# Layer 0's rows of sequences 3 to 7 turned by 32x32 blocks on VectorE and an exchange through memory

## The chip, the cores and the metric

The kernel runs on one core of a Trainium2 chip. The time is the device time of one execution in microseconds (us); of several runs the median is given. A trace of one profiled execution stands beside it: every instruction of the five engines (TensorE or PE, VectorE or DVE, ScalarE or ACT, GpSimd or POOL, SyncE or SP) with its start, its length and what it waited for. DMAs are issued from the queues of SyncE, ScalarE and GpSimd ("SPq", "ACTq", "POOLq" in the trace). All data are 32-bit floats.

## What is computed

Eight sequences (B = 8) of 128 positions with 512 features go through two layers. Layer 0 multiplies each sequence by an adapter matrix that its id picks, and adds a feed-forward step with two of eight low-rank experts. Layer 1 is attention over a paged cache of 512 keys plus the 128 new ones (32 query heads, 8 key heads, with normalised and rotated queries and keys), followed by a gated low-rank feed-forward step with 16 of 64 experts.

```python
x = x + _L0_ffn_ref(_L0_cond_ref(x, L0_cond_weight, itok_B_3_7), ...)
x = x + _L1_ffn_ref(_L1_cond_ref(x, L1_cond_Wq, L1_cond_Wk, L1_cond_Wv, L1_cond_Wo, ...), ...)

# in _L1_cond_ref
q = jnp.einsum('bsd,ed->bse', x, Wq).reshape(bsz, seqlen, HQ, D)
k = jnp.einsum('bsd,ed->bse', x, Wk).reshape(bsz, seqlen, HK, D)
v = jnp.einsum('bsd,ed->bse', x, Wv).reshape(bsz, seqlen, HK, D)
```

The change concerns what lies between the two layers: the projections of layer 1 (these three products) need x with the features on the partitions, and layer 0 leaves it with the positions on the partitions. So each sequence's 128x512 result has to be turned (transposed) once.

## The kernel before

**The order of the work is written by hand.** On each engine, and in each DMA queue, instructions run in the order in which the source issues them. An instruction that waits holds up all behind it in the same queue. Semaphores between queues are set by the framework from the reads and writes of tiles; a tile that takes a buffer of a pool waits until the last reader of the tile before it in that buffer is through.

**Layer 0** is the loop `for t in range(B)` from line 585. Iteration t computes the adapter product of sequence t (`l0_adapter`, lines 486 to 504, into PSUM and by `cT` on ScalarE back to SBUF), finishes the experts of sequence t-1 (`l0_turn_low` and `l0_experts`, lines 549 to 571, where L558 on TensorE needs `lowT`, which ScalarE copies from PSUM) and starts the base product of sequence t (`l0_base`, L512 and L517, which need `cT`). `l0_experts` leaves two things: the rows `x1` go to memory (L561, read again at the end of the kernel), and the rows scaled by a power of two go into the tile `xb` (L568 on ScalarE). `l0_turn` (lines 573 to 579), called two iterations later for t from 2 to 7 and twice after the loop, turns `xb` with four transposes on TensorE (L577) into a PSUM bank (`bank("q")`, for the last two sequences one of `banks`) and copies it on ScalarE into the operand tile `xo` (L579). The pool of `xb` has three buffers, so `l0_load_x(t + 2)` (L392, from the queue of SyncE) takes the buffer of sequence t-1.

From iteration 4 on, products of layer 1 (`project_whole`, L292) stand between those of layer 0 wherever their operands are there: for sequences 0 and 1 in the loop, for sequence 2 after it and in iteration 0 of layer 1, for sequence 3 from iteration 1. Sequences 4 to 7 enter through `sums_x` (GpSimd, iterations 2 and 5). `project_whole` puts its result into bank "q" or "kv", and ScalarE copies it out (L299). `norms` (ScalarE, with two steps on GpSimd), `rotate` (VectorE, lines 317 to 350) and `transpose_qk` (TensorE, L358) make queries and keys of the first units; `sums_q` (VectorE, L163) combines weights. SyncE's queue carries the loads of x, of weights and of key pages (`gather`, L194), and the writes of `x1`.

**Layer 1** is `for u in range(NU + 3)` with 64 units (a sequence and a key head each). Iteration u computes scores of unit u (L798, L801), a masked minimum and exponent (L811 on VectorE, L822 on ScalarE), a normalisation (L828 on GpSimd) and a turn of the probabilities by 32x32 blocks on VectorE (L833). `exchange_out` writes the blocks to memory from the queues of SyncE and ScalarE, `exchange_in` in the next iteration reads them back, so that blocks from different partitions change places; `values` (L880) uses them in iteration u+2, `evict_o` (L891) and `output` (L902) follow in iteration u+3. Queries and keys of unit 3 and later go the same way (L784, `px<-xo` and `qkb<-px`).

The pool `yp` (tag "ya", three buffers) holds `bias`, `ang` and `kk` in layer 0 and output rows in layer 1.

Of the kernel before, what the change touches and what calls it, by code (L numbers as in the profile page):

```python
# [9 lines left out]
F32 = mybir.dt.float32  # L10
# [6 lines left out]
P = 128  # L17
B = 8
S = 128
DM = 512  # L20
NC = DM // P
# [12 lines left out]
QD = P // 32  # L34
# [23 lines left out]
def adaln_ffn_kernel(  # L58
# [25 lines left out]
    nc = tc.nc  # L84
# [262 lines left out]
    def rotate(u):  # L347
        rotate_q(u)
        rotate_k(u)
# [14 lines left out]
        qkT_t[u] = home.rearrange("p (h s) -> p h s", h=NH)  # L364


    with ExitStack() as l0:
        w0p = l0.enter_context(tc.tile_pool(name="w0p", bufs=1))
        p2 = l0.enter_context(tc.tile_pool(name="l0_2", bufs=2))
# [25 lines left out]
        glw = w0p.tile([P, NC, E0 + E0 * R0], F32, name="glw")  # L395
        bww = w0p.tile([P, NC, DM], F32, name="bww")
        lb = w0p.tile([P, DM], F32, name="lb")
        bias = yp.tile([P, DM], F32, tag="ya", name="bias")

        wt_home = {}  # L400
        pairs = [wp.tile([P, 7, 2 * HW], F32, tag="wqkv", name=f"wqkv_{i}", bufs=GH) for i in (0, 1)]
# [171 lines left out]
        def l0_turn(b):  # L573
            x1 = state.pop(b)
            tp = banks(f"x1tp_{b}") if b >= B - 2 else bank("q", f"x1tp_{b}")
            for c in range(NC):
                nc.tensor.transpose(tp[:, c * S : (c + 1) * S], x1[:, c * P : (c + 1) * P], ident)  # L577
            half = xo[:, b // 2, b % 2 * 2 : b % 2 * 2 + 2]
            nc.scalar.copy(half.rearrange("p x c s -> p (x c s)"), tp[:, :DM])  # L579


        idle = bank("q", "idle")
# [2 lines left out]
        for t in range(B):  # L585
            l0_adapter(t, True)
            if t >= 1:
                l0_turn_low(t - 1)
            l0_adapter(t, False)
            if t + 3 < B:  # L590
                l0_load(t + 3)
            if t + 2 < B:
                l0_load_x(t + 2)
            if t in (3, 4):
                load_q(t - 3)
            if 2 <= t <= 5:
                gather(0, (t - 2) * 4, (t - 1) * 4)
            elif t > 5:
                gather(1, (t - 6) * 4, (t - 5) * 4)
            if t >= 2:  # L600
                l0_turn(t - 2)

            if t == 5:
                project_whole(0, 0, 0, 1)
                norms(0)
            if t == 6:
                project_whole(0, 0, 1, 0)
            if t == 7:
                project_whole(0, 1, 1, 1)
                transpose_qk(0)  # L610
            if t >= 1:
                l0_experts(t - 1)
            l0_base(t)
            if t == 0:
                l0_rows()
            if 1 <= t <= 4:
                l0_angles(t - 1)
            if t in (3, 6):
                gather_v(t // 3 - 1, 0, LC)
            if t in (5, 6):  # L620
                make_tables(t - 5)
            if t == 4:
                project_whole(0, 0, 0, 0)
            if t == 5:
                project_whole(0, 0, 1, 1)
                sums_q(0, 3, 2)
            if t == 6:
                project_whole(0, 1, 0, 1)
                rotate(0)
                norms(2)  # L630
                sums_q(0, 4)
            if t == 7:
                project_whole(0, 1, 0, 0)
                norms(1)
        for g in range(GH):
            load_o(g)
        l0_turn_low(B - 1)
        project_whole(0, 1, 1, 0)
        l0_turn(B - 2)
        rotate(1)  # L640
        l0_experts(B - 1)
        project_whole(1, 0, 0, 0)
        transpose_qk(1)
        norms(3)
        rotate(2)
        l0_turn(B - 1)
        project_whole(1, 0, 0, 1)
        transpose_qk(2, wt_7.rearrange("p c n -> p (c n)")[:, : NH * S])
        rotate(3)


    fw_t, zg_t = {}, {}
# [99 lines left out]
    with ExitStack() as l1:  # L752
# [223 lines left out]
        def iteration(u):  # L976

            on = lambda v: 0 <= v < NU
            fb = LAST.get(u)
            r, group = u % 16, (u // 16 + 1) * GH  # L980
            f = room(fb) if fb is not None else None

            if u % 4 == 3:
                k, j, four = (u + 5) // 4, 0, True
            elif u % 4 == 0:
                k, j, four = (u + 4) // 4, 0, False
            elif u % 4 == 1:
                k, j, four = (u + 3) // 4, 1, True
            else:
                k, j, four = (u + 2) // 4, 1, False  # L990
            slots = ()
            if 2 < u and k < NU // 4:
                slots = (1, 2, 6) if four else (4, 5, 3)
            st = u // GH
            pages = on(u) and 1 < st + 1 < NQ * B
            first, end = ((0, 10), (10, NPP))[u % GH]
            if pages:
                gather(st + 1, first, first + 3)
            if on(u - 1):
                exchange_in(u - 1)  # L1000
            if pages:
                gather(st + 1, first + 3, end)
            if pages:
                gather_v(st + 1, u % GH * LC // GH, (u % GH + 1) * LC // GH)
            if on(u + 3) and u % GH == 1:
                make_tables(units[u + 3][0])
            if u % GH == 0 and B <= st - 1 < NQ * B:
                load_y(st - 1)
            if on(u - 3):
                evict_o(u - 3)  # L1010
            if u >= NU and fb is not None:
                yT_t[fb] = f_turn(fb, *f)
            if u > NU:
                z = u - NU - 1
                z_turn(z, bank("q" if z else "kv", f"ztp_{z}"), lambda n, shape: y_home[
                    z
                ].rearrange("p (c s) -> p c s", c=NC))
            for h in range(REP):
                if on(u):
                    scores(u, h)  # L1020
                    mask_exp(u, h)
                    if h > 0:
                        normalize(u, h - 1)

                    if h == 1:
                        if u == 2:
                            rotate(4)
                        elif u == 3:
                            sums_q(1, 3, 2)
                        elif u == 4:  # L1030
                            sums_q(1, 4, 1)
                        elif r in (10, 11, 12, 13) and u < NU - 8:
                            sums_q(group + r // 12, *((3, 2), (4, 1))[r % 2])
                    if h == 2:
                        new_pb(u)
                        if u + 2 in range(3, NU):
                            blocks_qk(u + 2, u)
                    if h > 1:
                        blocks(u, h - 2)
                    if h == 1 and u == NU - 5:  # L1040
                        f_fold(f[1])
                    if h == 2 and fb is not None:
                        yT_t[fb] = f_turn(fb, *f)
                if on(u - 3):
                    output(u - 3, h)
                if h > 0 and slots:
                    project(k, j, slots[h - 1 : h])

                if (u, h) in WHOLE:
                    project_whole(1, *WHOLE[u, h])  # L1050
            if on(u - 3):
                add_output(u - 3)
            if on(u + 1) and (u + 1) % GH == 0:
                make_mask(units[u + 1][0])
            if u + 1 in range(3, NU):
                heads_qk(u + 1)

            if u < NU - 8:
                if r in (8, 9, 10, 11):
                    load_q(group + r // 10, r % 2, r % 2 + 2)  # L1060
                if r in (12, 13):
                    load_o(group, r % 2 * 2, r % 2 * 2 + 2)
            if 16 < u < NU and r in (1, 2):
                load_o(group - 1, r * 2 - 2, r * 2)
            if NU - 8 < u < NU - 2:
                f_weights(u - NU + 7)
            if u == 2:
                sums_q(0, 1)
            if on(u):
                normalize(u, REP - 1)  # L1070
            if u == 0:
                norms(4)
            elif 4 < u + 3 < NU:
                norms(u + 3)
            if on(u):
                blocks(u, REP - 2)
                blocks(u, REP - 1)
                exchange_out(u)
            if 4 < u + 3 < NU:
                rotate(u + 3)  # L1080
                if four and slots:
                    project(k, j, (7,))

            if u in (2, 5, 7, 9):
                sums_x({2: 2, 5: 3, 7: 0, 9: 1}[u])
            if u == NU - 14:
                t = wp.tile([P, 4 * DM], F32, tag="wo", name="y_home", bufs=GH + 1)
                y_home.update({b: t[:, b * DM : (b + 1) * DM] for b in range(4)})
            if u == NU - 6:
                rooms()  # L1090
            if fb is not None:
                f_gate(fb, *f_project(fb, yT_t.pop(fb), *f), *f)
            if on(u - 2):
                values(u - 2)
# [160 lines left out]
```

## Time and profile before

| what | value |
|---|---|
| median of three runs | 1243.18 us (1242.82 to 1249.42) |
| the profiled execution's own time | 1245.7 us |
| its span, first to last instruction | 1243.9 us |
| mean granted TensorE clock | 0.998 |
| moved by DMA | 298.99 MB, mean 240 GB/s |
| four transposes of one sequence (L577), each | 273 ns median |
| ScalarE's copy of one turned sequence (L579) | 592 ns median |
| layer 0's loop and tail | from the start to about 114 us |

"Busy" is the time in which an engine works on an instruction. TensorE's instructions are pipelined: a transpose is listed with 273 ns, though in a row of four the next one starts well before that. So the cost of a row of matmuls is read from its start to the start of what follows. The granted clock is the share of TensorE's full speed.

### The profile page before, as it was taken

Reading aid. Unit: us, or ns where it says so; the run is one execution under the profiler, and the core shown is the slowest. Engines: PE = TensorE matmul, PEld = TensorE weight load, DVE = VectorE, ACT = ScalarE, POOL = GpSimd, SP = SyncE. Lnnn points to the kernel's source line nnn. Section 1 sums busy time; section 2 is a strip of 40 time slices with the busy share of each in tenths; the row PEclk is TensorE's granted clock in tenths of the full one; section 3 lists DMA queues with packets and bytes.
Section 4 is the critical chain, followed back from the end, with each engine's and each line's share of the span. In section 5 each row is a group of like instructions: output and inputs, shape, how many; then the busy total and the mean of one; then the engine's idle time right before and its main releaser. Section 6 shows DMA issues by size and latency. Waiting matters only on the chain.

```text
span 1243.9 us, 15998 instructions
## 1 busy us (share of the span) xinstructions
PE 1225.7 (99%) x3847; PEld 651.1 (52%) x3847; DVE 901.9 (73%) x2045; ACT 506.5 (41%) x1457; POOL 590.9 (48%) x687
## 2 busy tenths in 40 slices
PE   8999899999999999999999999999999999999998
PEld 7765455554555555545555545554555555555444
DVE  3546788888877777788877777788777777777522
ACT  1334444444444444444444444444444444443211
POOL 2443565576544444565545545555555444543100
PEclk9999999999999999999999999999999999999999
DMA  8822777788877887788878878888888877787512
GB/s 302 304 78 94 229 234 245 245 274 281 269 243 245 272 258 239 259 295 278 269 248 267 264 221 258 294 272 267 257 268 262 255 243 233 246 261 269 179 51 85
DMA packets 205505, 298.99 MB, mean 240 GB/s; under 512 B 84643, under 2 KB 117156, under 8 KB 204516
## 3 DMA queue, kind: packets, MB, share of 16 engines
q1 hardware_dynamic: 173812, 205.58, 52.6%
q10 hardware_dynamic: 18720, 52.32, 12.0%
q0 software_dynamic: 12880, 40.08, 9.7%
q8 instruction: 31, 0.51, 0.2%
q14 instruction: 62, 0.51, 0.1%
HBM read 183.54 MB, written 114.36 MB: 239 GB/s over the span
## 4 chain that ended last, share of the span: by engine, by line
PE 89%; DMA 4%; DVE 2%; ACT 1%; issue 1%; POOL 1%; SPq 1%; ACTq 0%; DVEq 0%; POOLq 0%
PE o L880 19%; PE p L259 19%; PE y L902 17%; PE s L798 16%; PE s L801 4%; PE bp L517 2%; PE op L1147 2%; PE p L292 2%; PE cp L495 2%; PE fz L701 2%; DMA kt<-in_kc 1%; DMA bww<-in_base_w 1%; DMA px<-pb 1%; PE cp L512 1%; DMA pT<-px 1%
## 5 line engine op out<-in xcount | busy, mean ns | idle before, releaser
L828 POOL TENSOR_SCALAR p<-p,den 128x640 f32<-128x640 f32 x256 | 211.8, 827 | 424.4 <-DVE den L827 423.8
L822 ACT ACTIVATE p<-p,low 128x640 f32<-128x640 f32 x256 | 211.9, 828 | 436.3 <-DVE den L827 295.6
L811 DVE CUSTOM_DVE_ANT_0 p<-s,mask,rs 128x640 f32<-128x640 f32 x256 | 223.5, 879 | 108.8 <-PE s L801 106.1
L259 PE MATMUL p<-wqkv,xo 128*128 128x384 f32 x784 | 280.5, 487 | 0.0
L902 PE MATMUL y<-wo,oT 128*128 128x512 f32 x512 | 262.8, 598 | 7.6 <-ACT oT L891 7.4
L798 PE MATMUL s<-kt,qkT 128*128 128x512 f32 x504 | 258.9, 595 | 1.5 <-DVE low L811 0.8
L880 PE MATMUL o<-pT,vt 128*128 128x512 f32 x512 | 230.2, 593 | 0.0
L833 DVE STREAM_TRANSPOSE pb<-p 128x640 f32<-128x640 f32 x256 | 211.0, 824 | 16.9 <-POOL p L828 16.9
L259 PEld LDWEIGHTS p<-wqkv,xo 128*128 128x128 f32 x784 | 149.1, 190 | 139.8 <-issue 72.3
L801 PEld LDWEIGHTS s<-qkT 128*128 128x128 f32 x504 | 96.2, 191 | 121.0 <-issue 121.0
L880 PEld LDWEIGHTS o<-pT,vt 128*128 128x128 f32 x512 | 97.5, 190 | 110.1 <-issue 95.0
L204 POOL DMA_INDIRECT vt<-in_vc,vrow x128 | 136.3, 1065 | 37.4 <-issue 28.2
L798 PEld LDWEIGHTS s<-kt,qkT 128*128 128x128 f32 x504 | 95.4, 191 | 96.7 <-issue 54.0
L308 ACT ACTIVATE sq<-c 128x128 f32<-128x128 f32 x320 | 98.8, 309 | 8.1
L314 POOL TENSOR_TENSOR rs<-ss,mhalf 128x5 f32<-128x5 f32 x64 | 99.5, 1554 | 5.3
L801 PE MATMUL s<-qkT 128*128 128x128 f32 x504 | 97.2, 275 | 0.0
L891 ACT COPY oT<-o 128x512 f32<-128x512 f32 x64 | 37.4, 585 | 144.9 <-PE o L880 133.6
L902 PEld LDWEIGHTS y<-wo,oT 128*128 128x128 f32 x512 | 78.6, 192 | 14.2 <-ACT oT L891 9.7
L262 DVE TENSOR_TENSOR c<-c,p 128x384 f32<-128x384 f32 x84 | 45.3, 539 | 28.8 <-PE p L259 28.7
L880 PE MATMUL o<-pT,vn 128*128 128x512 f32 x128 | 65.4, 592 | 0.0
L308 ACT ACTIVATION_READ_ACCUMULATOR sq<-c 128x1 f32 x320 | 59.7, 187 | 0.0
L340 DVE SCALAR_TENSOR_TENSOR ca<-c,rs,tab 128x128 f32<-128x128 f32 x64 | 24.8, 387 | 45.1 <-POOL rs L314 45.1
(181 smaller groups left out, 1200.7 us busy)
## 6 DMA issues: line engine op xcount, KB each, us to landing
pT<-px SPq DMA_DIRECT2D x64, 1280.0 KB, 6.7
px<-pb ACTq DMA_DIRECT2D x120, 400.0 KB, 5.3
px<-pb SPq DMA_DIRECT2D x120, 400.0 KB, 5.5
qkb<-px SPq DMA_DIRECT2D x61, 320.0 KB, 3.5
kt<-in_kc SPq DMA_DIRECT2D x512, 32.0 KB, 4.4
wqkv<-in_wqkv POOLq DMA_DIRECT2D x32, 384.0 KB, 5.4
yd<-ya SPq DMA_DIRECT2D x24, 256.0 KB, 3.1
wo<-in_wo POOLq DMA_DIRECT2D x12, 512.0 KB, 4.7
```

The source lines that it names most:

```text
L204: nc.gpsimd.indirect_dma_start(out=kv_t[step][1][:, c, :], out_offset=None, in_=vc, in_offset=bass.IndirectOffsetOnAxis(ap=vrow[:, hf, at ...
L259: nc.tensor.matmul(out=ps, lhsT=xo[:, pr, x, c, :], rhs=w[:, c, :], start=(c == 0), stop=(c == 1))
L308: nc.scalar.activation(sq, cs[:, at : at + D], AF.Square, accum_out=ss[:, h : h + 1])
L314: nc.gpsimd.tensor_tensor(rs, ss, mhalf, ALU.pow)
L798: nc.tensor.matmul(out=s[:, :L], lhsT=qkT[:, h, :], rhs=kt[:, :, g % GH, :], start=True, stop=True)
L801: nc.tensor.matmul(out=s[:, L:NK], lhsT=qkT[:, h, :], rhs=qkT[:, REP, :], start=True, stop=True)
L811: nc.vector.tensor_tensor_reduce(out=p, in0=s_t.pop((u, h))[:, :NK], in1=mask_t[st], scale=rs_t[u][:, h : h + 1], scalar=BIG, op0=ALU.add, ...
L822: nc.scalar.activation(p, p, AF.Exp, bias=low, scale=-1.0, accum_out=den)
L828: nc.gpsimd.tensor_scalar(p_t[u, h], p_t[u, h], den, 1.0, ALU.mult, ALU.mult)
L833: nc.vector.transpose(pb_t[u][:, :, h * w : (h + 1) * w].rearrange("p i (j a) -> p j i a", a=32), p_t.pop((u, h)).rearrange("p (j i a) -> ...
L880: nc.tensor.matmul(out=o, lhsT=vt[:, c, j * D : (j + 1) * D] if c < LC else vn_t.pop(u), rhs=pT[:, c], start=(c == 0), stop=(c == LC),)
L902: nc.tensor.matmul(out=y_t[st], lhsT=oT_t[u][:, h, :], rhs=wo_t[g][:, h, :], start=(h == 0 and j == 0), stop=(h == REP - 1 and j == GH - 1),)
```

## The change

Sequences 0, 1 and 2 are turned as before. For sequences 3 to 7, `l0_turn` is replaced by four steps:

- `l0_blocks(b)`: one VectorE transpose of the 128x512 rows by blocks of 32x32 into a buffer of `yp` (`turn_blocks`), and four DMA writes of it to memory from SyncE's queue (`turn_out`), one for each group of 32 partitions.
- `l0_read(b)`: one DMA read, again from SyncE's queue, which brings the blocks to their partitions (`turn_in`).
- `l0_chunks(b)`: one copy on ScalarE that puts the pieces in order into `xo` (`turn_chunks`).

In iteration t of layer 0 the read of sequence t-2 (from t = 5) stands where `l0_turn` stood, behind the loads and gathers of that iteration in SyncE's queue; the blocks of sequence t-1 (from t = 4) and then the copy of sequence t-2 (from t = 5) stand at the iteration's end. After the loop, the read of sequence 6 takes the place of its turn, and the blocks of sequence 7 come after the last `rotate(3)`. Layer 1's iteration 0 issues the read of sequence 7, ahead of that iteration's `exchange_out`; the copies of 6 and 7 stand in iterations 1 and 2, behind head 2. `bias` moves from `yp` into a buffer of its own, so that `yp` has a free buffer. The buffer of `xb` is now free after the block transpose. On TensorE, 20 transposes are gone; on VectorE there are 5 block transposes more; ScalarE has five copies from SBUF in place of five from PSUM; SyncE has 25 DMAs more.

```diff
--- before.py
+++ after.py
@@ -364,6 +364,41 @@
         qkT_t[u] = home.rearrange("p (h s) -> p h s", h=NH)
 
 
+
+    def turn_blocks(rows, room):
+        nc.vector.transpose(
+            room.rearrange("p (k c a) -> p c k a", k=QD, c=NC),
+            rows.rearrange("p (c k a) -> p c k a", c=NC, k=QD),
+        )
+
+    def turn_out(n, room):
+        m = dram.tile([QD, 32, QD, NC * 32], F32, name=f"yx_{n}")
+        for i in range(QD):
+            nc.sync.dma_start(
+                out=m[:, :, i].rearrange("k b f -> b k f"),
+                in_=room[i * 32 : (i + 1) * 32].rearrange("p (k f) -> p k f", k=QD),
+            )
+        return m
+
+    def turn_in(m, room):
+        nc.sync.dma_start(
+            out=room.rearrange("p (i f) -> p i f", i=QD), in_=m.rearrange("k b i f -> (k b) i f")
+        )
+
+    def turn_chunks(out, room):
+
+        nc.scalar.copy(
+            out.rearrange("p c (i a) -> p c i a", a=32),
+            room.rearrange("p (i c a) -> p c i a", i=QD, c=NC),
+        )
+
+    rows_t = {}
+
+    def operand(b):
+
+        return xo[:, b // 2, b % 2 * 2 : b % 2 * 2 + 2].rearrange("p x c s -> p (x c) s")
+
+
     with ExitStack() as l0:
         w0p = l0.enter_context(tc.tile_pool(name="w0p", bufs=1))
         p2 = l0.enter_context(tc.tile_pool(name="l0_2", bufs=2))
@@ -395,7 +430,7 @@
         glw = w0p.tile([P, NC, E0 + E0 * R0], F32, name="glw")
         bww = w0p.tile([P, NC, DM], F32, name="bww")
         lb = w0p.tile([P, DM], F32, name="lb")
-        bias = yp.tile([P, DM], F32, tag="ya", name="bias")
+        bias = w0p.tile([P, DM], F32, name="bias")
 
         wt_home = {}
         pairs = [wp.tile([P, 7, 2 * HW], F32, tag="wqkv", name=f"wqkv_{i}", bufs=GH) for i in (0, 1)]
@@ -575,8 +610,18 @@
             tp = banks(f"x1tp_{b}") if b >= B - 2 else bank("q", f"x1tp_{b}")
             for c in range(NC):
                 nc.tensor.transpose(tp[:, c * S : (c + 1) * S], x1[:, c * P : (c + 1) * P], ident)
-            half = xo[:, b // 2, b % 2 * 2 : b % 2 * 2 + 2]
-            nc.scalar.copy(half.rearrange("p x c s -> p (x c s)"), tp[:, :DM])
+            nc.scalar.copy(operand(b), tp[:, :DM].rearrange("p (c s) -> p c s", c=NC))
+
+        def l0_blocks(b):
+            room = yp.tile([P, DM], F32, tag="ya", name=f"xr_{b}")
+            turn_blocks(state.pop(b), room)
+            rows_t[b] = turn_out(f"x{b}", room), room
+
+        def l0_read(b):
+            turn_in(*rows_t[b])
+
+        def l0_chunks(b):
+            turn_chunks(operand(b), rows_t.pop(b)[1])
 
 
         idle = bank("q", "idle")
@@ -597,8 +642,10 @@
                 gather(0, (t - 2) * 4, (t - 1) * 4)
             elif t > 5:
                 gather(1, (t - 6) * 4, (t - 5) * 4)
-            if t >= 2:
+            if 2 <= t < 5:
                 l0_turn(t - 2)
+            if t >= 5:
+                l0_read(t - 2)
 
             if t == 5:
                 project_whole(0, 0, 0, 1)
@@ -632,21 +679,25 @@
             if t == 7:
                 project_whole(0, 1, 0, 0)
                 norms(1)
+            if t >= 4:
+                l0_blocks(t - 1)
+            if t >= 5:
+                l0_chunks(t - 2)
         for g in range(GH):
             load_o(g)
         l0_turn_low(B - 1)
         project_whole(0, 1, 1, 0)
-        l0_turn(B - 2)
+        l0_read(B - 2)
         rotate(1)
         l0_experts(B - 1)
         project_whole(1, 0, 0, 0)
         transpose_qk(1)
         norms(3)
         rotate(2)
-        l0_turn(B - 1)
         project_whole(1, 0, 0, 1)
         transpose_qk(2, wt_7.rearrange("p c n -> p (c n)")[:, : NH * S])
         rotate(3)
+        l0_blocks(B - 1)
 
 
     fw_t, zg_t = {}, {}
@@ -1002,6 +1053,9 @@
                 gather(st + 1, first + 3, end)
             if pages:
                 gather_v(st + 1, u % GH * LC // GH, (u % GH + 1) * LC // GH)
+
+            if u == 0:
+                turn_in(*rows_t[B - 1])
             if on(u + 3) and u % GH == 1:
                 make_tables(units[u + 3][0])
             if u % GH == 0 and B <= st - 1 < NQ * B:
@@ -1031,6 +1085,8 @@
                             sums_q(1, 4, 1)
                         elif r in (10, 11, 12, 13) and u < NU - 8:
                             sums_q(group + r // 12, *((3, 2), (4, 1))[r % 2])
+                    if u in (1, 2) and h == 2:
+                        turn_chunks(operand(B - 3 + u), rows_t.pop(B - 3 + u)[1])
                     if h == 2:
                         new_pb(u)
                         if u + 2 in range(3, NU):
```

## The prediction

> **What bounds the kernel.** I read the page's busy shares first, then the timeline of each engine between 56 and 150 us (the stage that is edited), then the chain of waits behind it. Columns of a timeline: start us, us, engine, line, what, and in brackets the idle time before it with its releaser. The page:
>
> ```profile
> PE 1225.7 (99%) x3847; PEld 651.1 (52%) x3847; DVE 901.9 (73%) x2045; ACT 506.5 (41%) x1457; POOL 590.9 (48%) x687
> PE 89%; DMA 4%; DVE 2%; ACT 1%; issue 1%; POOL 1%; SPq 1%; ACTq 0%; DVEq 0%; POOLq 0%
> ```
>
> TensorE is busy for 1225.7 of 1243.9 us and makes up 89% of the chain, so a microsecond taken from its queue in layer 0 counts in full, as far as no later wait takes it back. TensorE's timeline round two of the five turns:
>
> ```profile
> 75.40 0.60 PE L577 MATMUL x1tp<-ident,xb 128*128 128x128 f32 x4
> 76.72 2.85 PE L292 MATMUL p<-wqkv,xo 128*128 128x384 f32 x8 [0.73 <-ACT xo L579]
> 79.41 1.02 PE L558 MATMUL bp<-lb,lowT 128*128 128x512 f32 x2
> ...
> 109.54 0.71 PE L358 MATMUL tq<-ident,ca 128*128 128x128 f32 x5
> 111.09 0.66 PE L577 MATMUL x1tp<-ident,xb 128*128 128x128 f32 x4 [0.84 <-ACT xb L568]
> 111.58 2.75 PE L292 MATMUL p<-wqkv,xo 128*128 128x384 f32 x8
> ```
>
> A turn is short, but two of them carry a wait: turn 4 holds bank q until ScalarE has emptied it, turn 7 waits for the scaled rows. Now the queue of SyncE, and the operations of VectorE and ScalarE that bear on it:
>
> ```profile
> 76.06 0.34 SPq L392 DMA_DIRECT2D xb<-in_x  x1
> 76.91 2.84 SPq L194 DMA_DIRECT2D kt<-in_kc  x4
> 79.84 0.38 SPq L561 DMA_DIRECT2D x1d<-x  x1
> ```
>
> ```profile
> 70.98 2.23 DVE L163 TENSOR_TENSOR wqkv<-wqkv 128x768 f32<-128x768 f32 x2
> ```
>
> ```profile
> 73.81 0.27 ACT L554 COPY lowT<-ltp 128x128 f32<-128x128 f32 x1 [1.42 <-PE ltp L552]
> ```
>
> The load of xb 7 is issued at 76.06, just after turn 4 (75.40), because it takes the buffer of xb 4. Issues stand in one queue, so all behind it is late too. The chain of waits (start us, us, what) further on:
>
> ```profile
> 140.83 4.71 DMA px<-xo
> ...
> 146.21 6.56 DMA pT<-px
> ...
> 153.14 0.59 ACT oT L891
> ...
> 153.78 1.50 PE y L902 x2
> ```
>
> Here, in iteration 3, the chain leaves TensorE: TensorE stands 2.61 us (its timeline, before L902 at 153.78) for the exchange of units 0 and 1. A shift that TensorE has before this point counts only if the exchange has it as well. The stage after that stand, in columns stretch, length, busy time of PE, PEld, DVE, ACT, POOL, then clock, DMA share, GB/s:
>
> ```profile
> 153.70:158.40 4.70, 4.62 (x9) 2.21 (x10) 4.67 (x7) 0.47 (x2) 3.99 (x6) 0.64 1.00 232
> ```
>
> The granted clock is 0.64 there, against 1.00 in the stretches around it: 4.7 x 0.36 = 1.7 us lost.
>
> **Removed: 20 transposes (4 for each of sequences 3 to 7).** Start to start of the successor: turn 3 0.44 (60.90 to 61.34), turn 4 1.32 (75.40 to 76.72, wait included), turns 5 and 6 0.43 each (90.89 to 91.32, 105.67 to 106.10), turn 7 about 1.4 (end of tq near 110.2 to 111.58). Sum 4.0 us, the most that can be gained on TensorE. The Trainium skill, "VectorE: DVE Perf Modes", section "The three transpose paths" and its rules for authors, speaks against this edit: a full 128x128 turn belongs on TensorE if PSUM will do, since VectorE turns blocks of 32x32 only. Its figure of 390 ns a transpose (for bf16) would make 20 x 0.39 = 7.8 us removed; the trace has 0.44 us for four in a row, 2.2 us without the waits. I take the trace. The other half of the rule holds: what the blocks leave undone must go through memory.
>
> **Added on VectorE: five block transposes 128x512.** Nearest row: L833, 824 ns for 128x640, so 0.66 us each (bounds 0.6 to 0.85). The first four lie in VectorE's idle stretches (8.9 us before 65.03, 7.3 before 80.52, 6.2 before 95.57, 2.4 before 102.96): nothing, while that cover is there. The fifth stands after rotate(3) and ahead of the first mask: 0.66 us in the path of unit 0.
>
> **Added on ScalarE:** five copies 128x512 in place of five from PSUM (587 ns; the SBUF row L867 has 710 ns for 128x640): the count is equal, the place is not. Copy 3 now stands at the end of iteration 5, ahead of lowT 5 and cT 6, for which TensorE waits; copy 5 stands ahead of lowT 7.
>
> **Added on SyncE: 20 writes and 5 reads.** Issue 0.35 to 0.45 us each (px<-pb, x1d). Read landing: nearest rows of 256 KB:
>
> ```profile
> xb<-in_x SPq DMA_DIRECT2D x8, 256.0 KB, 3.0
> ya<-yd SPq DMA_DIRECT2D x24, 256.0 KB, 3.2
> ```
>
> I take 3.0 to 3.2 (bounds 2.0, the quickest yd row, and 7.5, the slowest kt). A write: 4 to 6.5 us (px rows), hidden, as the read comes an iteration later, except for 6 and 7, where SyncE itself waits.
>
> **The new wait.** In SyncE's queue, read 3 stands behind the load of xb 7 and four gathers, and that load now waits for the block transpose of 4, which stands behind sums_q on VectorE. All with turn 3 gone (-0.44): sums_q ends at 70.98 + 2.23 - 0.44 = 72.8; transpose 4 ends at 73.4; xb 7 and the gathers take 79.84 - 76.06 = 3.8 until the next issue, so read 3 goes out at 77.2 and lands at 80.3. ScalarE holds copy 3 until then: to 80.9, then lowT 5 to 81.1. TensorE's L558, which would come at 79.41 - 0.44 - 1.32 = 77.65, comes at 81.15: a stall of 3.5 us, 1.7 later than before. Queued behind it on ScalarE are cT 6 (81.5, needed at 82.0: covered) and a copy of p.
>
> **The clock after that stall.** The Trainium skill, "TensorE: Matmul & The Clock Gate", section "Part 1: The HAM clock gate", says that an idle window of about 3.4 us, free-running, halves the clock until the next busy one. By the rule a 3.5 us gap seldom fills a whole window, and costs nothing; the row above fell to 0.64 after 2.61 us of idling, so the window need not be empty. At the start of the run 1.57 us of idling (before 8.02) left the clock at 1.00. I put 2 in 3 on a dip, for another 1.7 us.
>
> **What follows to iteration 3.** Without the dip, TensorE is at +1.7; turn 5 gives -0.43; turn 6 gives its 0.43, which copy 5 ahead of lowT 7 takes back; turn 7 gives 1.4, but rotate(3) still waits for norms(3), which stand on ScalarE behind tq 1 (late by 1.7 - 0.43, about 1.2): its line L340, at 116.18 before, comes at 116.9, and rotate(3) ends 0.7 late, near 118.35. Transpose 7 ends at 119.0. SyncE then issues 4 writes (1.7), 8 gathers (0.84 apart, 6.7 with the first's preparation), read 7 (0.4): free at 127.95. The exchange of unit 0, issued at 126.82 before, would be ready on VectorE's side at +0.9; so SyncE sets it, +1.1. DMA is at 99% of its share in 127 to 134, so the 256 KB of read 7 ahead of it add 0.26 MB / 380 GB/s = 0.7. The exchange is 1.8 late, and with it pT of unit 0, the last px<-xo (which waits for it), pT of unit 1 and L902. TensorE's own lateness (0.9) is inside the stand. With the dip all of it is 1.7 later: +3.5. From there on the order on all engines is that of before, and the shift stays.
>
> **The sum.** The profiled execution took 1245.7 (span 1243.9 and 1.8 around it), 2.5 above the median of the three runs, 1243.18. 1245.7 + 3.5 = 1249.2 for a profiled one; on the median 1243.2 + 3.5 = 1246.7.
>
> **Rivals.**
> - No dip of the clock: the same sum without 1.7: 1245.0. For it: the rule's full window; against it: the row with 0.64.
> - The transfer is hidden: read 3 lands before ScalarE comes to copy 3. Then TensorE has -2.2 until turn 7, and the whole end of layer 0 is 3.4 earlier than in the case above: rotate(3) ends near 115.0, the exchange goes out at 124.6, +0.7 for read 7: -1.6, 1241.6. Not -4.0, as SyncE's queue sets iteration 3. For it: DMA share is 0.27 between 72 and 87, so reads are quick; against it: the issue itself stands behind 3.8 us of queue.
> - Slower by over 0.5%: read 3 lands late. Each microsecond past 3.1 is a microsecond of stall; from a landing of 3.1 + 6.2 - 3.5 = 5.8 us the loss passes 0.5%. qkb rows reach 4.2, yd 6.4, kt 7.5, under load; this stretch has little load. At 6.5 us: 1250.1.
> That the change doesn't take place is ruled out: the built order has 20 transposes fewer on TensorE.
>
> **Chances.** The forecast with the dip 0.47; no dip 0.25; hidden 0.15; late landing 0.13. The likeliest gives 1246.7. 0.5% (6.2 us) is about what a measurement of this kernel can tell from no change. Faster by more would need a gain above the 4.0 that there is: 0.01. Slower by more: the late landing's chance and a little for a longer dip: 0.14. The range goes from the hidden case, 1241.4, to 1250.6 (forecast plus the late landing's bound at 6.5 us and noise).
>
> **What would show it.** TensorE: 3827 matmuls; a gap before L593 (the old L558) of iteration 6 near 77.6, released by ScalarE's lowT, which itself waited for a DMA xr<-yx; a clock below 1.00 in the 4 us after it. SyncE: xb 7 at 73.5, read 3 near 77.2. A gap near 3.5 us confirms the new wait; none, with the copy of 3 not waiting, would refute it. The exchange of unit 0 leaving SyncE near 128 (129.7 with the dip), right behind read 7, would confirm that it sets iteration 3; if it leaves when VectorE is ready, the queue is innocent. Wrong altogether if the steady part after 170 us changes its pace.

## The result, and the profile after

| | before | after |
|---|---|---|
| median of nine runs each | 1245.44 us (1241.68 to 1249.42) | 1250.38 us (1246.9 to 1254.28) |
| ratio after / before, 95% interval | | 1.0044 (1.0025 to 1.0063) |
| the profiled execution's own time | 1245.7 us | 1254.28 us |
| its span | 1243.9 us | 1252.5 us |

The kernel became slower, by 0.0044 x 1245 = 5.5 us (3.1 to 7.8); the two medians differ by 4.9 us. The prediction said 3.5 us slower, and put 0.85 on a change within 0.5%, which it held too small to be told from none. The profiled execution of after is the longest of its nine runs, so its trace shows more than the median does, and three more traces of the same kernel are used below.

The page's busy shares and the chain's shares, after:

```profile
PE 1228.6 (98%) x3827; PEld 650.0 (52%) x3827; DVE 905.6 (72%) x2050; ACT 506.4 (40%) x1457; POOL 589.4 (47%) x687
PE 82%; DMA 3%; DVE 3%; ACT 2%; POOL 1%; issue 1%; ACTq 1%; SPq 1%; DVEq 0%; POOLq 0%
```

The 20 transposes are gone (3847 to 3827 matmuls), and yet TensorE is busy 2.9 us longer: some of the work that stayed ran at a lower clock. Its share of the chain fell from 89% to 82%; the other engines now hold the end back more often. TensorE's timeline around iteration 6, with columns as in the prediction, shows where:

```profile
74.63 2.75 PE L292 MATMUL p<-wqkv,xo 128*128 128x384 f32 x8
80.74 2.08 PE L593 MATMUL bp<-lb,lowT 128*128 128x512 f32 x2 [3.37 <-ACT lowT L589]
...
84.42 4.86 PE L552 MATMUL bp<-bww,cT 128*128 128x512 f32 x8
89.11 2.74 PE L292 MATMUL p<-wqkv,xo 128*128 128x384 f32 x8
```

L593 is the old L558. It took 1.02 us for two matmuls before and takes 2.08 now, right after a gap of 3.37 us: half the speed. From L593 to the next L292 it is 89.11 - 80.74 = 8.37 us, where the trace of before has 84.62 - 79.41 = 5.21:

```profile
84.62 2.75 PE L292 MATMUL p<-wqkv,xo 128*128 128x384 f32 x8
```

The first two rows below are the stretches of that time after the change (the granted clock is the third column from the end). The third row is the stage behind the stand of iteration 3 of layer 1, to which the text comes back further on:

```profile
80.70:84.40 3.70, 3.66 (x10) 2.63 (x11) 1.42 (x3) 0.86 (x2) 0.00 (x0) 0.50 0.22 54
84.40:87.60 3.20, 3.20 (x7) 1.42 (x6) 2.67 (x15) 0.91 (x2) 2.36 (x3) 0.60 0.57 168
...
160.10:164.10 4.00, 3.92 (x6) 1.85 (x7) 3.97 (x5) 0.03 (x1) 3.60 (x5) 0.50 0.99 231
```

In the first two rows the clock reads 0.50 and 0.60: 3.7 x 0.50 + 3.2 x 0.40 = 3.1 us lost, which is the 8.37 - 5.21 = 3.16. The releaser of the gap is ScalarE's `lowT`. ScalarE's timeline says what held that copy, VectorE's when the block transpose of sequence 4 ran, and SyncE's when the read that ScalarE waited for was issued:

```profile
79.90 0.62 ACT L390 COPY xo<-xr 128x512 f32<-128x512 f32 x1 [8.28 <-DMA xr<-yx_x]
80.43 0.26 ACT L589 COPY lowT<-ltp 128x128 f32<-128x128 f32 x1
```

```profile
72.37 0.70 DVE L369 STREAM_TRANSPOSE xr<-xb 128x512 f32<-128x512 f32 x1
```

```profile
73.14 0.36 SPq L427 DMA_DIRECT2D xb<-in_x  x1
74.00 2.85 SPq L194 DMA_DIRECT2D kt<-in_kc  x4
76.96 0.37 SPq L384 DMA_DIRECT2D xr<-yx_x  x1
...
131.71 0.37 SPq L384 DMA_DIRECT2D xr<-yx_x  x1
132.43 0.81 SPq L898 DMA_DIRECT2D px<-pb  x2
```

This is the new wait, step by step as forecast: the load of xb 7 (73.14) waits for the block transpose (over at 73.07), four gathers follow, and only then read 3 goes out (76.96, forecast 77.2). It lands 2.92 us later (forecast 3.0 to 3.2). ScalarE, idle for 8.28 us, then copies, and `lowT`, which had its data long before, comes behind that copy. The last two rows show the second new limit: SyncE issues the exchange of unit 0 right behind read 7. Before, SyncE had nothing to issue in the 9 us ahead of that exchange:

```profile
126.82 0.82 SPq L847 DMA_DIRECT2D px<-pb  x2
```

This limit is a close one. VectorE's last blocks for the exchange are ready at 131.86, and before the change SyncE issued 0.13 us after that point; so its queue delays the exchange by 0.44 us, and VectorE would have set it at 131.99.

One step was not foreseen. Under `rotate(3)`, the GpSimd step that VectorE's L340 waits for, and beside it VectorE:

```profile
118.35 1.26 POOL L312 TENSOR_SCALAR ss<-ss,eps 128x5 f32<-128x5 f32 x1 [3.01 <-ACT sq L308]
```

```profile
118.26 0.69 DVE L326 TENSOR_TENSOR ca<-c,tab 128x512 f32<-128x512 f32 x1 [0.91 <-ACT sq L308]
118.87 0.69 DVE L326 TENSOR_TENSOR sa<-c,tab 128x512 f32<-128x512 f32 x1
```

In the trace of before the first of these products began 0.83 us after L312, behind it:

```profile
114.14 0.27 POOL L312 TENSOR_SCALAR ss<-ss,eps 128x5 f32<-128x5 f32 x1 [2.49 <-ACT sq L308]
```

```profile
114.97 0.69 DVE L326 TENSOR_TENSOR ca<-c,tab 128x512 f32<-128x512 f32 x1 [1.91 <-PE tq L358]
```

VectorE waited there for `tq` of unit 2 on TensorE, and turn 7 stood ahead of that. With turn 7 gone, `tq` comes about 0.9 us earlier against ScalarE's `norms(3)`, and the two meet. (After the change `tq` ends at 118.17, when the last `sq` of ScalarE is through as well, and the bracket names `sq`.) The chain's end in this stage, after:

```profile
146.98 5.07 DMA px<-xo
...
152.72 6.45 DMA pT<-px
...
159.54 0.60 ACT oT L942
...
160.18 2.07 PE y L953 x2
```

All four steps are those of before, 6.2 to 6.5 us later; here the loss of layer 0 passes into layer 1.

**A measure for comparing traces.** Traces of the same kernel differ by up to 2.4 us in the start of layer 0's iteration 5. So the "net shift" below is: the start of `oT` (ScalarE) of unit 0 or unit 1, minus that of before (153.14 and 171.90), minus the difference that L593 of iteration 5 already has (63.92 before), minus the 0.44 us of turn 3, which lies ahead of that line. It is what the edit has cost by the time that iteration 3 of layer 1 ends. For the first trace: 159.54 - 153.14 + 0.77 - 0.44 = 6.7 us at unit 0, and 7.6 at unit 1.

### The profile page after: what moved, and what is told of

It reads as the page before. It is cut to its first block, busy times and chain, and to the rows that moved or that the text cites. A ratio compares the mean times of both kernels' runs of the same rounds, so it can differ in the third digit from the quotient of the medians.

```text
span 1252.5 us, 15989 instructions
## 1 busy us (share of the span) xinstructions
PE 1228.6 (98%) x3827; PEld 650.0 (52%) x3827; DVE 905.6 (72%) x2050; ACT 506.4 (40%) x1457; POOL 589.4 (47%) x687
## 4 chain that ended last, share of the span: by engine, by line
PE 82%; DMA 3%; DVE 3%; ACT 2%; POOL 1%; issue 1%; ACTq 1%; SPq 1%; DVEq 0%; POOLq 0%
PE o L931 19%; PE p L259 19%; PE y L953 17%; PE s L849 16%; PE s L852 4%; PE op L1203 2%; PE fz L752 2%; DMA px<-pb 1%; DMA pT<-px 1%; ACTq L898 1%; PE bp L552 1%; PE p L292 1%; ACT sq L308 1%; POOL p L879 1%; DVE pb L884 1%
## 5 line engine op out<-in xcount | busy, mean ns | idle before, releaser
L340 DVE SCALAR_TENSOR_TENSOR ca<-c,rs,tab 128x128 f32<-128x128 f32 x64 | 24.9, 389 | 43.3 <-POOL rs L314 43.3
```

## The experiments

The theory: the copy that waits on ScalarE makes the gap, the gap lowers the clock, and SyncE's queue carries the delay into the exchange. The rivals: the read's lateness as such, the added work alone, or something in the steady part of layer 1. "Ratio" is against the kernel before on the same chip. Kernels of one batch ran on one chip; batches on different ones, so ratios are compared, not times.

**e1_read_first: the read ahead of the iteration's loads.**

```diff
             l0_adapter(t, False)
+            if t >= 5:
+                l0_read(t - 2)
             if t + 3 < B:
                 l0_load(t + 3)
...
-            if t >= 5:
-                l0_read(t - 2)
```

> The read of the turned blocks stands ahead of the loads and gathers of its iteration in SyncE's queue; everything else as in the changed kernel. Theory (the read issued late, behind the load of xb 7, makes ScalarE wait with lowT 5 behind it): read 3 goes out near 66 us instead of 76.96, the gap of 3.37 us on TensorE before L593 of iteration 6 is gone, the clock of 80.7 to 87.6 is 1.00 instead of 0.50 to 0.60, and the ScalarE copy of unit 0's values (oT), at 159.54 in the changed kernel and 153.14 before, comes near 153; time 5 to 6.5 us under the changed kernel, so about 1244 to 1245, no faster than before by more than 2. Rival (the added DMA traffic and issues or the block transposes themselves cost the time): the time stays within 2 us of the changed kernel's 1250.4.

Measured: 1245.66 us, ratio 1.0009 (0.9995 to 1.0022). SyncE's and TensorE's timelines:

```profile
66.88 0.34 SPq L384 DMA_DIRECT2D xr<-yx_x  x1
```

```profile
78.03 1.02 PE L593 MATMUL bp<-lb,lowT 128*128 128x512 f32 x2
...
83.25 2.74 PE L292 MATMUL p<-wqkv,xo 128*128 128x384 f32 x8
```

Read 3 goes out 10 us earlier, L593 has no gap, and L593 to L292 takes 5.22 us as before. Net shift 0.1 us at both units. So the loss comes from the place of the read: one move in the queue takes the ratio from 1.0044 to 1.0009.

But where is the gain of the removed turns? TensorE does have it: the last L593 of layer 0 comes at 104.45, against 106.10 before; with the differences at iteration 5, 2.1 us earlier. Then it is given back in pieces. GpSimd's L312 takes 1.31 us here as well, and VectorE's L340 comes 2.62 us after its start where it came 2.04 (+0.6). Block transpose 7 stands ahead of the first mask (+0.7). Unit 0's exchange, behind read 7 (125.92, the exchange at 126.64), takes 7.40 us from its first write to its reading back where it took 6.84 (+0.6). -2.1 + 0.6 + 0.7 + 0.6 = -0.2; the trace has +0.1.

**e2_copy_later: the copies of 3, 4 and 5 one iteration later, the read left where it is.**

```diff
-            if t >= 5:
-                l0_chunks(t - 2)
+            if t >= 6:
+                l0_chunks(t - 3)
...
-                    if u in (1, 2) and h == 2:
+                    if u in (0, 1, 2) and h == 2:
```

> The queue of SyncE is that of the changed kernel, read 3 goes out near 77 again, but ScalarE's copies of 3, 4 and 5 stand one iteration later (5 in layer 1's iteration 0), where their data have long landed. Theory (it is the copy waiting on ScalarE with lowT 5 and cT 6 behind it that stops TensorE, not the late read as such): no gap before L593 of iteration 6, clock 1.00, time as in the kernel with the early read, 1244 to 1245. Rival (SyncE's late queue delays something else as well): the gap goes but over half of the loss stays, 1248 or more.

Measured: 1246.19 us, ratio 1.0014 (1.0003 to 1.0026). SyncE's and TensorE's timelines:

```profile
77.47 0.37 SPq L384 DMA_DIRECT2D xr<-yx_x  x1
```

```profile
77.70 1.02 PE L593 MATMUL bp<-lb,lowT 128*128 128x512 f32 x2
```

The read is as late as in the kernel after, and the gap is gone all the same (next L292 at 82.92, 5.22 us). Net shift -0.5 and +0.6. So a late read costs nothing by itself; the copy that waits for it ahead of `lowT` on ScalarE does.

**e3_warm: 32 transposes of the identity, results unused, in TensorE's queue ahead of L593 of iteration 6.**

```diff
+            if t == 6:
+                warm = bank("o", "warm")
+                for i in range(WARM):
+                    nc.tensor.transpose(warm[:, :S], ident, ident)
             if t >= 1:
                 l0_experts(t - 1)
```

> 32 transposes of the identity into an idle bank stand in TensorE's queue ahead of L593 of iteration 6; the wait of ScalarE is as in the changed kernel. They take about 32 x 0.11 = 3.5 us, so L593 comes at 80.7 to 81.5. Theory (about half of the loss is the half-speed clock after the stand): the stand is filled, the clock of the next 7 us is 1.00, L593 to the next L292 takes 5.2 us instead of 8.4, time 2.5 to 3.2 us under the changed kernel, 1247.5. Rival (the slow stretch has another cause, such as DMA traffic): the stretch stays at 8 us and the time at 1250 or above.

Measured: 1248.33 us, ratio 1.0033 (1.0021 to 1.0045). TensorE's timeline:

```profile
77.52 3.66 PE L661 MATMUL warm<-ident 128*128 128x128 f32 x32
81.08 1.13 PE L593 MATMUL bp<-lb,lowT 128*128 128x512 f32 x2
...
86.41 2.74 PE L292 MATMUL p<-wqkv,xo 128*128 128x384 f32 x8
```

L593 is just as late (17.62 us after that of iteration 5; 17.59 in the kernel after, 15.49 before), but what follows takes 5.33 us. The wait is kept and the clock's fall is gone. Net shift 3.1 at both units, against 5.5 as the mean of four traces of the kernel after (6.2 at unit 1). The ratios agree: 1.0009 without the wait, 1.0033 with the wait at full clock, 1.0044 with both. The first step (0.0024, 3.0 us) is clear of the noise, though only just; the second (0.0011, 1.4 us) is not, and rests on the traces.

**e5_blocks7_first: block transpose of 7 ahead of `rotate(3)`, all else as after.**

```diff
-        rotate(3)
         l0_blocks(B - 1)
+        rotate(3)
```

> The block transpose of sequence 7 stands ahead of rotate(3) on VectorE instead of behind it. Theory (rotate(3) began 0.9 us earlier relative to norms(3) than before, and its two-operand multiplications held up GpSimd's step on the sums, 1.26 us instead of 0.27; the transpose behind it adds 0.7 to the path to the first mask and to SyncE's queue): the transpose falls into VectorE's idle time at 117.3 to 118.3, GpSimd's step takes 0.27 or at most 0.8, the first mask comes 0.7 to 1.7 earlier relative to L593, time 1 to 1.7 us under the changed kernel, about 1249. Rival (the exchange of iteration 0 is bound by something later than the queue of SyncE): the mask comes earlier but the time stays at 1250.4.

Measured: 1250.03 us, ratio 1.0048 (1.0028 to 1.0068). L312 still took 1.25 us, so the part of the theory that this order would keep GpSimd and VectorE apart missed. Read 7 now goes out at 124.60 and the exchange at 129.20, 4.6 us behind it: SyncE no longer sets it, VectorE does. The total gained nothing that the interval can tell. TensorE's timeline holds a surprise:

```profile
81.77 1.13 PE L593 MATMUL bp<-lb,lowT 128*128 128x512 f32 x2 [3.37 <-ACT lowT L589]
...
87.09 2.74 PE L292 MATMUL p<-wqkv,xo 128*128 128x384 f32 x8
```

The same gap of 3.37 us, and 5.32 us behind it: no fall of the clock in this execution. With it missing, this trace has a net shift of only 1.4, while the timed runs lie 6 us (3.5 to 8.5) above before. Whether those runs did have the fall, no trace shows, and the distance between the two figures stays open.

**after_look_2, after_look_3, after_look_4: the kernel after, three more traces.** No edit.

> The changed kernel again, for one more trace. Theory (the clock's fall after the gap before L593 [...]differs between executions of one kernel): the gap is 3.3 to 3.5 us again, and the time from L593 of iteration 6 to the next L292 is somewhere between 5.2 (no fall) and 8.4 us (as in the first trace); over several traces its mean excess is about 2 us. Rival (the fall is fixed by the program): 8.4 us in each trace.

> As for the second look: gap 3.3 to 3.5 us; L593 to the next L292 between 5.2 and 8.4 us by the theory[...], 8.4 us by the rival.

> As for the second look: gap 3.3 to 3.5 us; L593 to the next L292 between 5.2 and 8.4 us by the theory[...], 8.4 us by the rival.

Measured (gap before L593; L593 to the next L292, less the 5.21 of before; net shift at units 0 and 1):

| trace | gap | the clock's cost | net shift |
|---|---|---|---|
| first | 3.37 us | 3.2 us | 6.7, 7.6 us |
| look_2 | 3.53 us | 1.8 us | 5.2, 6.2 us |
| look_3 | 3.29 us | 1.7 us | 5.5, 5.5 us |
| look_4 | 3.24 us | 1.8 us | 4.5, 5.5 us |

TensorE's timeline of look_2, the one with the longest gap:

```profile
83.31 1.12 PE L593 MATMUL bp<-lb,lowT 128*128 128x512 f32 x2 [3.53 <-ACT lowT L589]
...
90.31 2.10 PE L292 MATMUL p<-wqkv,xo 128*128 128x384 f32 x6
```

L593 itself runs at full speed (1.12), the fall comes in what follows: 7.00 us in all. The fall varies from execution to execution of one kernel, and the first trace had an unusually long one. L312 took 1.26 to 1.29 us in all of them, so that collision is a fixed part of the cost. Unit 0's exchange goes out 0.7 us behind read 7 in all four.

**e9_turns_kept: the exchange as in e1, and the old turns too, from which all operands come; the exchanged data are not used.**

```diff
-            turn_blocks(state.pop(b), room)
+            turn_blocks(state[b], room)
...
-            if 2 <= t < 5:
+            if 2 <= t:
                 l0_turn(t - 2)
...
-            if t >= 5:
-                l0_chunks(t - 2)
```

> The early-read kernel with all turns kept on TensorE as before; the block transposes, the writes and the reads stay, but nothing uses what they bring (ScalarE's five copies of it are left out, the output is unchanged). It has all of the added work and none of the removal. Theory (the added work costs only what stands in the path of iteration 0: block transpose 7 behind rotate(3), SyncE's queue, the traffic of read 7): the oT copy of unit 0 comes 1 to 2.5 us later than before, time near 1246.5, so the removal of 20 transposes is worth 1 us or less where the early-read kernel has 1245.7. Rival (the removal brings its 4.0 us and the traffic takes them back everywhere): time near 1249.

Measured: 1249.41 us, ratio 1.0038 (1.002 to 1.0056). Net shift 1.7 and 2.0 us: by the trace the added work alone costs 2 us, by the times 4.7 (2.5 to 7.0). By the trace it is the theory's figure, by the times the rival's; the two don't agree, and that stays open. Against e1, removing the turns is worth 1.6 to 1.9 us by the traces and 3.6 (0.8 to 6.4) by the ratios; only the traces speak against the full 4.0 that they take on TensorE. In this trace SyncE's queue holds the exchange back more than in the kernel after: VectorE's blocks are ready at 127.43, the exchange goes out at 128.83. With the turns back, L312 took 0.27 us: turn 7 had kept VectorE's products away from it.

**e1n, e1b, e1nb: on top of e1, `norms(3)` ahead of the last experts, block transpose 7 ahead of `rotate(3)`, or both.**

```diff
         rotate(1)
+        norms(3)
         l0_experts(B - 1)
...
-        norms(3)
...
-        rotate(3)
         l0_blocks(B - 1)
+        rotate(3)
```

> The early-read kernel with norms(3) ahead of the last experts on ScalarE, where ScalarE idles 3.5 us. Theory (with turn 7 gone rotate(3) waits for norms(3), whose step on GpSimd takes 1.26 us under rotate(3)'s multiplications instead of 0.27): rotate(3) loses its 1.4 us wait for rs, the first mask comes 1.4 to 2 us earlier than in the early-read kernel (117.30), but SyncE's queue behind block transpose 7 moves with it; oT of unit 0 near 152, time 1.5 us under the early-read kernel, about 1244. Rival (the exchange is bound elsewhere): oT of unit 0 stays at 153.8.

> The early-read kernel with block transpose 7 ahead of rotate(3). Theory: the first mask comes 0.7 earlier (116.6), SyncE is through with read 7 five us before the exchange, so that VectorE sets it; oT of unit 0 1 to 2 us earlier than in the early-read kernel, time 1244 to 1245. Rival (VectorE's path sets the exchange in both): oT of unit 0 comes by 0.7 earlier only and the time moves by 0.7 or less.

> The early-read kernel with both: norms(3) early and block transpose 7 ahead of rotate(3). Theory: the first mask near 115.1 instead of 117.30, the exchange of unit 0 near 124.4 and set by VectorE, oT of unit 0 near 151.3, 1.8 us ahead of the kernel before; time 1242.5 to 1243.5, the first that is under both kernels. Rival (iteration 3 is bound by something that no step of layer 0 moves): oT stays near 153 and the time at 1244.6 or above.

| kernel | L312 | unit 0's exchange | net shift, units 0 and 1 | ratio (interval) |
|---|---|---|---|---|
| e1 | 1.31 us | 126.64 | 0.1, 0.1 us | 1.0009 (0.9995 to 1.0022) |
| e1n | 0.28 us | 125.63 | -1.3, -0.5 us | 0.9994 (0.998 to 1.0007) |
| e1b | 1.24 us | 125.67 | -1.9, -0.8 us | 1.0004 (0.999 to 1.0018) |
| e1nb | 0.27 us | 124.57 | -2.1, -0.8 us | 0.9998 (0.9983 to 1.0013) |

GpSimd's step in the kernel with both:

```profile
107.40 0.27 POOL L312 TENSOR_SCALAR ss<-ss,eps 128x5 f32<-128x5 f32 x1 [0.37 <-ACT sq L308]
```

Now it starts 1.67 us before VectorE's next products (109.07, those of `rotate(2)`) and is short again. With the difference at iteration 5 taken off, the exchange goes out 1.5, 1.3 and 2.4 us earlier than in e1: the two corrections together bring more than either alone, but not their sum. None of the four ratios is told from another. And from unit 0 to unit 1 1.3 us are lost again, as the windows behind iteration 3's stand show (the first row is of e1nb, the second of before):

```profile
152.40:156.40 4.00, 3.92 (x6) 1.86 (x7) 3.96 (x5) 0.03 (x1) 3.60 (x5) 0.50 1.00 232
...
153.70:157.70 4.00, 3.92 (x7) 1.98 (x8) 3.97 (x5) 0.02 (x1) 3.59 (x5) 0.59 1.00 231
```

TensorE stands 2.49 us here, little less than before (2.61), and the clock that follows is lower: 0.50 in these 4 us and 0.73 in the next 4, against 0.59 and 0.99 in the same 8 us of before. That is 0.36 + 1.04 = 1.4 us. In e1nb another stand, of 1.57 us, lies 1.3 us ahead of this one, where before has 0.49. Whether the earlier exchange makes the slow stretch longer is not shown: in the four traces of the kernel after, one program, the second 4 us have a clock of 0.80 to 1.00.

**e1nbw_warm_u3: 22 transposes of the identity, results unused, in that stand.**

```diff
+                if u == 3 and h == 0:
+                    warm = bank("kv", "warm")
+                    for i in range(22):
+                        nc.tensor.transpose(warm[:, :S], ident, ident)
                 if on(u - 3):
                     output(u - 3, h)
```

> The kernel with the early read, norms(3) early and block transpose 7 first, and 22 transposes of the identity into an idle bank in TensorE's stand of iteration 3 (2.5 us, ahead of the first output product). Theory (what the earlier exchange gains there, 1.3 us, is lost again to a longer slow clock after the stand): the clock stays at 1.00 after the stand, the first output product comes at about 152.5 as without them, and the oT copy of unit 1 comes at 170.0 instead of 171.9; time 1 to 2 us under that kernel, near 1243. Rival (the slow stretch there is no matter of idling, or the total wanders by more than this): unit 1 at 171.9 or the time at 1245 or above.

Measured: 1244.89 us, ratio 0.999 (0.9975 to 1.0006). The same window:

```profile
152.40:156.40 4.00, 3.93 (x12) 2.04 (x12) 3.97 (x5) 0.02 (x1) 3.60 (x5) 1.00 0.99 234
```

The clock stays at 1.00, `oT` of unit 1 starts at 168.99 (expected 170.0), and the net shift is -2.5 and -4.1 us. It holds, as a difference to the trace of before, up to about unit 26 of 64; at the last unit it is +0.4. The time is not clearly below before. By the net shift this is the best version of the study; by the time no gain is shown.

## Why the mechanism was right, and the size and the chances were not

The forecast named the new wait, its place and its length, and a loss of 3.5 us; but it put 0.85 on a change within 0.5% as one that can't be told from none, and the loss of 5.5 us (3.1 to 7.8) is clear of zero. The step that failed is the path through `rotate(3)`, which the sum had 0.7 us late and which came 1.9 us late, 1.0 of it from a GpSimd step that the sum took at its old duration. The clock's term was too small as well. The steps of the prediction, against the traces of the kernel after:

- **The wait of TensorE: right.** Gap 3.5 forecast, 3.24 to 3.53 measured; L593 later by 1.7, or by 2.2 counted from iteration 5 (17.7 instead of 15.49 us), measured 17.46 to 17.76. The cause is the one named: e1 removes it at the read, e2 at the copy.
- **Turns 5 and 6: right.** From L593 of iteration 7 to the last one it is 11.66 us, against 11.65 before: turn 6's gain was taken back by the wait for copy 5 (0.28 us of idling). Turn 5 gave 0.29 (forecast 0.43).
- **The clock after the stall: right in kind, short in size.** 1.7 us forecast; 3.2, 1.8, 1.7 and 1.8 measured, 2.1 in the mean. This term was taken from one row, the stage behind the stand of 2.61 us, and given no spread. The rule of the Trainium skill that was weighed there ("TensorE: Matmul & The Clock Gate", "Part 1: The HAM clock gate": an idle window of about 3.4 us) would have made it nothing for gaps of 3.24 to 3.37, which are shorter than the window. Three such gaps cost 1.7 to 3.2 us here, and one cost 0.1. The stand of 2.49 in e1nb, with the shorter one ahead of it, left the clock at 0.50. The measurement decides: a gap shorter than the rule's window can halve the clock. Another sentence of that section says that the window is free-running and that the number of slow matmuls at a kernel's start varies from run to run for that reason; the cost here, behind a gap within the kernel, varied from execution to execution too, though no run shows that a window is the reason. A single row was no size, but one draw.
- **`rotate(3)`: the step that failed.** The prediction had it end 0.7 late, with GpSimd's step at its old duration. In the first trace it ends at 122.46 instead of 117.71; with the differences at iteration 5 that is 5.1 us late, and 1.9 without the 3.16 of the clock. With turn 7 gone, VectorE's L326 starts in time to run beside GpSimd's L312, and that takes 1.26 us for 0.27: +1.0, in all four traces. e9, with turn 7 back, and e1n, with `norms(3)` earlier, both give 0.27 again. It could have been read from the trace of before: the two steps stood 0.83 us apart and are released by different engines, and the edit moves one against the other by about 1 us. What happens when such steps meet stood there as well, 4 us earlier: GpSimd's L570, which otherwise takes 0.26 us, took 1.33 beside the products of `rotate(2)`, which started at 110.33 and 110.92 (it held nothing up there):

```profile
110.32 1.33 POOL L570 TENSOR_SCALAR eps<-up 128x1 f32<-128x1 f32 x1 [1.97 <-DVE up L567]
```

- **The exchange of unit 0: right.** From the end of block transpose 7 to SyncE's being free 9.0 us were forecast and 132.08 - 123.08 = 9.0 measured. Not counted: SyncE needs another 0.35 us until the exchange's first write; so it sets the exchange 0.44 us behind VectorE, where the forecast had 0.2. Read 7 ahead of it: 0.7 forecast, and (139.89 - 132.43) - 6.84 = 0.6 measured. One reading behind that term was wrong: the share of the DMA engines between 127 and 134 is 0.67 in the trace of before, not 99%; only from 128 to 132 is it 0.93 to 1.01.
- **The stage behind iteration 3: not foreseen, small.** The forecast let the shift stay from there. Unit 1 shows another 0 to 1.0 us from the clock behind the stand.

Together, at unit 0: 3.5 + 0.4 (clock, mean) + 1.0 (GpSimd) + 0.35 (SyncE) = 5.25 us, against a mean net shift of 5.5 in the four traces and 5.5 (3.1 to 7.8) by the ratio. That the three agree so well is in part luck: single traces have 4.5 to 6.7, and the interval is wide. 1250.38 lies just within the range given, at its upper end; but the median of before rose as well, by 2.3 us from three runs to nine, and as a difference the range went from -1.8 to +7.4 us, with 4.9 measured.

The chances were the other weak point. 0.85 stood on "within 0.5%", with 0.5% named as what a measurement of this kernel can tell. The interval turned out as +-0.19%, so a loss of 0.44% is told from no change, though most of that interval lies within the band. The rivals "hidden" and "no dip" fell: there was a gap in all traces of the kernel after, and a fall of the clock in all four. "Late landing" fell too: 2.92 us in the first trace. "No dip" is seen only in one trace of e5.

Where the expected 4.0 us went: with the wait removed (e1), TensorE is 2.1 us ahead at the last experts. GpSimd's collision, block transpose 7 and read 7 in the queue take this back before unit 0's exchange, and turn 7's share is hidden behind `norms(3)`. In its trace, what e1nb wins back there is lost to the clock behind iteration 3's stand, and only with that stand filled (e1nbw) is the whole stage about 4 us ahead.

## What to carry to other kernels

A detour through memory needs its read ahead of unrelated loads in the queue, and the copy that uses it late enough to find the data there; an engine that works in order holds everything behind a copy that waits, and here one read placed 10 us too late cost 3 us of gap and about 2 us of lowered clock. Price a gap on TensorE with its clock, as a range, and fill it with idle transposes if it can't be closed (worth 2.4 us here by the traces of e3, too little to show in its times). Before work is taken off the busiest engine, follow the gain to the next point at which another engine or queue sets the time, and look at what starts earlier there and with what it will then collide.

## What the runs showed that was not expected

- A GpSimd operation on 128x5 elements took 1.24 to 1.31 us instead of 0.27 when two VectorE products of 128x512 ran beside it (0.69 us each, back to back): it was held for as long as both of them. The Trainium skill ("SBUF — State Buffer", "SBUF: two separate sides") says that VectorE with two inputs and GpSimd share a port pair which the one that starts first locks for its whole instruction. In the trace L326 starts 0.09 us ahead of L312, which agrees; that the hold spans two VectorE instructions in a row is what these runs add. Who is first could not be told where the starts lie closer: L570 (L605 after the change), listed 0.01 to 0.08 us ahead of L326, took 1.33 us in the trace of before, 0.81 in the first of after and 0.27 in e1.
- Executions of one kernel drift apart in the steady part of layer 1 by 1.5 us to several, in jumps at about units 24 to 33, 41 to 46 and 54 to 56; look_4 had the smallest net shift at unit 0 and, with 1260.2 us, the longest time. No run here says what the jumps are. They are a likely reason, not a shown one, why net shifts and ratios don't always agree (e5, e9, e1nbw). The prediction had named a change of pace after 170 us as the sign of being wrong altogether. Against the trace of before, from unit 1 to the last unit, the four traces of after lose 1.3, 1.9, -0.8 and 8.0 us, and those of the other variants -2.2 to 6.0: nothing in this sets the change apart.
